# A cross-attention kernel with its instructions in another order: a new table of turns, and a scheduler whose turns need not follow its clock

## The chip, the core and the metric

The kernel runs on one core of one Trainium2 chip. A core has five engines that each work through their own list of instructions in order: TensorE (PE, with its weight loads shown apart as PEld), VectorE (DVE), ScalarE (ACT), GpSimd (POOL) and SyncE (SP, here the main issuer of transfers). They wait for each other through semaphores. The metric is the device time of one execution in microseconds (us). The kernel before has 572.43 us as the median of three runs (572.14 to 574.06).

## The reference

Two attention branches over the same rows are summed, projected and added to the input. `x` is (2, 2048, 640), `enc` (2, 128, 384), with 8 heads of 80 columns; all of it is fp32.

```python
residual = hidden_states                                  # x
enc, ca = encoder_hidden_states[:, :124], encoder_hidden_states[:, 124:]
hs = _mha(hidden_states @ Wq, enc @ Wk, enc @ Wv)         # text branch
ca_q1 = einsum('btc,th->bch', ca, Wq_ca)                  # (2, 384, 640)
ca_q1 = ca_q1[:, indices, :]                              # 2048 rows, 384 different ones
ca_hs1 = _mha(ca_q1, residual, residual)
ca_hs2 = _mha(ca_hs1 @ Wq, ca @ Wk_ca, ca @ Wv_ca)        # adapter branch, 4 tokens
out = (hs + ca_hs2) @ Wout + b_out + residual
```

## The kernel before

The rows are worked in 8 **blocks** of 512 rows (four for each of the two inputs) and 16 **units** of 256 rows. The stages overlap in time:

- **Queries** (`queries_fast`, PE tiles `pq`). The product x·Wq of a block is taken with fewer, larger products in the manner of Strassen: a chain of products accumulates in one PSUM bank, and after each product the running sum is read out and added to a quarter of `q`. Since the next product of a chain goes on in the same bank, it waits until the read of the step before has been done (`ready + at`). The reads are copies on ACT or DVE, or adds on DVE. A fifth column group (`pq_n_4`) is taken plainly; it is split into a rounded half and a rest (ACT cast to `x_sums`, DVE difference, ACT cast to `wq_sums`, DVE difference) and goes to DRAM and back (`away`, `landing`, `rests`).
- **Text scores** (PE tiles `sc`, DVE row maxima `m`, ACT exponentials `p`, transposes `eb`, then through DRAM as `kept` and back as `pT`).
- **The adapter branch**. Scores `s1` come as quads of matmuls into one buffer of four banks. DVE reduces it to maxima (`mx<-s`) and only then may the next quad write; later the scores are taken again (`s<-cop,zop`), ACT makes exponentials `ea`, and PE sums them (`acc<-ea,y_sb`). `y_sb` is x transposed by halves, written to DRAM (`y`) and read back in quarters on the SP queue. The branch ends in 384 rows `o2` for each input (`po2`), kept in DRAM.
- **Text out** (`text_out_fast`, PE tiles `ph` and `po`). For unit m, `ph_m_0`, `ph_m_2` and `ph_m_4` are copied out into `hs` (ACT or DVE), four sums s1 to s4 of parts of `hs` are made on DVE or POOL (s3 from the first copy, s1 from the first two, s2 from s1, s4 from s2), and four chains of products with Wout run in the banks `po_m_0` to `po_m_3`. Chain 0 has four steps. Each step is followed by a DVE add of the bank into the output rows (`x_more` or `last_rows`), and, as with the queries, the next step of a chain waits for that add.
- **Store**. POOL adds the rows of `o2` by an indirect transfer (line 2351), and the output rows are stored by SP or ACT.

An fp32 matmul appears in the trace as two records, so eight matmuls of a chain (two products of `by_columns`, line 405, over four groups of 32 columns) are 16 records.

**What sets the order.** The whole program is written out by a list scheduler, the class `Desk`. Tasks are generators that yield operations (`Do`): the engines that may do it, a function that emits instructions, the events to wait for, and the buffers it takes (`needs`) and gives back (`frees`). The table `TURNS` holds for every operation of every task a number; `run` always issues the operation with the least number, and the number modulo 6 names its engine in `ENGINES` (PE, ACT, DVE, POOL, SP, NONE). Instructions are pinned in this order. So the table alone sets the order on each engine, and where an operation may go to two engines, which one does it. The scheduler keeps a clock of its own with modelled durations (`ready`, `issue`, `streamed`); of that clock one thing reaches the program: which buffer of a set is taken, since the buffer that became free earliest is. What an engine waits for on the chip follows from the data and the buffers.

Of the kernel before, what the change touches and what calls it, by code (L numbers as in the profile page):

```python
# [14 lines left out]
P = 128  # L15
# [44 lines left out]
class Task:  # L60
    def __init__(self, gen, rank, key, more):
        self.gen, self.rank, self.key, self.more, self.last = gen, rank, key, more, Event()
        self.forks, self.ops, self.path = 0, 0, ""


class Desk:
# [242 lines left out]
    def begin(self, gen, rank):  # L309
        name = gen.__name__  # L310
        n = self.begun[name] = self.begun.get(name, -1) + 1
        task = Task(gen, rank, (name, n), 0.0)
        task.last.t = self.now
        self.parent.forks += 1
        task.path = f"{self.parent.path}.{self.parent.forks}"
# [2276 lines left out]
```

## Time and profile before

| | before |
|---|---|
| median of three runs | 572.43 us (572.14 to 574.06) |
| span of the profiled execution | 571.3 us |
| PE busy | 563.6 us, 99% |
| DVE busy | 394.4 us, 69% |
| ACT busy | 286.7 us, 50% |
| POOL busy | 159.8 us, 28% |
| PE clock granted | 9 of 10 or more in every slice |
| bytes moved | 113.21 MB, mean 198 GB/s |

The profiled execution spans 571.3 us, 1.1 us under the median of the runs. Times in the trace count from the start of that span. A row of a timeline gives the start, the length, the engine, the line, the tiles written and read, the shape and how many instructions of that kind came in a row; a bracket at its end gives the idle time ahead of it and what ended it. Matmuls are pipelined, so the length of a row of PE reaches past the start of the next, and the pitch from start to start is the better price. A short wait of PE can be hidden under the modelled ends.

### The profile page before, as it was taken

The page shows a single profiled execution, that of the slowest core. Times are in us where ns is not written, and L with a number is a line of the kernel's source. Part 1 is how long each engine was busy: PE and PEld are TensorE (multiplying, and loading weights), DVE is VectorE, ACT ScalarE, POOL GpSimd, SP SyncE. Part 2 cuts the span into 40 slices and gives each one's busy share as a digit, 9 for nine tenths or more (in the row PEclk, how much of TensorE's full clock was granted, in tenths as well). Part 3 has the DMA queues.
Part 4 walks back from the last instruction along what each step waited for, and adds up shares of the span by engine and source line. Part 5 has one row for each costly group of instructions (what it writes and reads, how often), then busy time and mean ns, then how long its engine had stood idle before and what let it go on. Part 6 is the DMA issues. An engine that isn't in the chain of part 4 may idle for free.

```text
span 571.3 us, 18875 instructions
## 1 busy us (share of the span) xinstructions
PE 563.6 (99%) x8069; PEld 310.0 (54%) x8069; DVE 394.4 (69%) x659; ACT 286.7 (50%) x806; POOL 159.8 (28%) x213
## 2 busy tenths in 40 slices
PE   9999999999999999999999999999999999999997
PEld 8885335455555455466554554554555554445553
DVE  4366999999998577458999999998332213544443
ACT  2021355645566899899876654524554664100000
POOL 9102041114440731100004350531203053045152
PEclk9999999999999999999999999999999999999999
DMA  8998576965968977446746969977476587799888
GB/s 246 211 248 126 139 161 157 172 179 139 211 212 153 215 182 211 146 126 198 233 158 203 316 180 319 245 217 230 96 263 120 164 206 223 248 211 213 258 156 237
DMA packets 145691, 113.21 MB, mean 198 GB/s; under 512 B 82548, under 2 KB 116980, under 8 KB 145608
## 3 DMA queue, kind: packets, MB, share of 16 engines
q1 hardware_dynamic: 137000, 95.10, 60.0%
q0 software_dynamic: 5632, 10.69, 11.7%
q10 hardware_dynamic: 2976, 6.23, 3.2%
q8 instruction: 63, 1.03, 0.8%
q14 instruction: 20, 0.16, 0.1%
HBM read 71.60 MB, written 40.39 MB: 196 GB/s over the span
## 4 chain that ended last, share of the span: by engine, by line
PE 92%; DVE 3%; ACT 3%; DMA 1%; issue 1%; SPq 0%; ACTq 0%; DVEq 0%
PE po L405 27%; PE pq L405 24%; PE sc L396 7%; PE acc L396 7%; PE s L396 7%; PE ph L396 6%; PE pq L396 4%; PE pyz L396 2%; ACT ea L427 2%; DVE mx L427 2%; PE pv L396 1%; PE pk L396 1%; DMA xz<-in_x_dram 1%; ACT p L427 1%; PE pt_wq L410 1%
## 5 line engine op out<-in xcount | busy, mean ns | idle before, releaser
L427 ACT ACTIVATE p<-sc,m 128x124 f32<-128x124 f32 x256 | 90.1, 381 | 43.4 <-DVE m L427 38.4
L427 DVE TENSOR_REDUCE mx<-s 128x4 f32<-128x2048 f32 x48 | 109.0, 2271 | 1.9 <-PE s L396 1.9
L427 ACT ACTIVATE ea<-s 128x2048 f32<-128x2048 f32 x48 | 90.5, 1884 | 31.4 <-PE s L396 30.9
L405 PE MATMUL po<-wout_sums,hs 128*32 128x320 f32 x1024 | 78.5, 434 | 0.1
L405 PE MATMUL po<-wout_sb,hs 128*32 128x320 f32 x928 | 72.4, 433 | 0.0
L427 POOL TENSOR_TENSOR p<-p,r 128x992 f32<-128x992 f32 x17 | 31.4, 1847 | 130.9 <-DVE r L427 130.9
L405 PE MATMUL pq<-xt,wq_sb 128*32 128x256 f32 (+1 forms) x928 | 66.4, 418 | 0.0
L427 DVE TENSOR_TENSOR last_rows<-last_rows,po 128x320 f32<-128x320 f32 x60 | 28.1, 480 | 44.0 <-PE po L405 43.9
L427 ACT ACTIVATION_READ_ACCUMULATOR p<-sc,m 128x1 f32 x256 | 57.0, 223 | 0.0
L427 DVE TENSOR_TENSOR x_more<-x_more,po 128x320 f32<-128x320 f32 x68 | 32.4, 481 | 34.5 <-PE po L405 32.5
L405 PEld LDWEIGHTS po<-wout_sums,hs 128*32 128x32 f32 x1024 | 33.4, 110 | 32.7 <-issue 2.8
L427 DVE TENSOR_REDUCE m<-sc 128x4 f32<-128x496 f32 x64 | 40.8, 663 | 14.1 <-PE sc L396 14.0
L396 PE MATMUL acc<-ea,y_sb 128*32 128x384 f32 (+2 forms) x768 | 50.2, 382 | 0.2 <-ACT ea L427 0.2
L396 PE MATMUL ph<-pT,vpad 128*32 128x256 f32 x768 | 47.9, 381 | 0.0
L405 PEld LDWEIGHTS po<-wout_sb,hs 128*32 128x32 f32 x928 | 30.1, 110 | 28.2 <-issue 1.6
L2351 POOL DMA_INDIRECT x_more<-o,query x17 | 26.6, 1563 | 67.0 <-DVE x_more L427 31.1
L405 PEld LDWEIGHTS pq<-xt,wq_sb 128*32 128x32 f32 x928 | 27.7, 110 | 28.0 <-issue 13.4
L427 ACT COPY hs<-ph 128x512 f32<-128x512 f32 (+1 forms) x25 | 13.4, 551 | 57.7 <-PE ph L396 57.7
L427 DVE STREAM_TRANSPOSE eb<-p 128x1024 f32<-128x1024 f32 x32 | 39.4, 1233 | 1.2 <-POOL p L427 1.1
L396 PEld LDWEIGHTS sc<-kmain,q 64*128 64x128 f32 x512 | 31.8, 187 | 12.6 <-issue 5.8
L427 POOL TENSOR_TENSOR hs<-hs 128x256 f32<-128x256 f32 x31 | 28.9, 1019 | 33.9 <-ACT hs L427 25.6
L396 PE MATMUL sc<-kmain,q 64*128 64x124 f32 x512 | 38.0, 285 | 0.0
(219 smaller groups left out, 835.0 us busy)
## 6 DMA issues: line engine op xcount, KB each, us to landing
kept<-eb SPq DMA_DIRECT2D x32, 512.0 KB
pT<-kept SPq DMA_DIRECT2D x16, 1024.0 KB
landing<-away SPq DMA_DIRECT2D x15, 512.0 KB
xi<-in_x_dram SPq DMA_DIRECT2D x56, 128.0 KB
x_more<-in_x_dram SPq DMA_DIRECT2D x17, 320.0 KB
last_rows<-in_x_dram SPq DMA_DIRECT2D x15, 320.0 KB
y<-yt SPq DMA_DIRECT2D x16, 256.0 KB
y_sb<-y SPq DMA_DIRECT2D x32, 128.0 KB
```

The source lines that it names most:

```text
L396: self.pin(self.nc.tensor.matmul(out, lhsT, rhs, **kw))
L405: self.pin(self.nc.tensor.matmul(out[j : j + 32], lhsT[:, j : j + 32], rhs, **kw))
L410: self.pin(self.nc.tensor.transpose(out, in_, ident))
L427: self.pin(getattr(engine, what)(*args, **kw))
L2351: desk.pin(nc.gpsimd.indirect_dma_start(out=t, out_offset=None, in_=o2_of[b], in_offset=bass.IndirectOffsetOnAxis(ap=query[:, st : st + 1] ...
```

## The change

The operations stay the same: PE has the same 4494 matmuls and transposes before and now, and no wait, copy or transfer is added in the code of any stage. Four things differ.

1. The table `TURNS` has other numbers for nearly every operation. The order of instructions changes on every engine, though the first 95 rows of PE (about the first 65 us) are the same. Some operations change engine: the sums of `hs` go from 31 on POOL and 33 on DVE to 37 and 27; the sums of `x_sums` from 17 on POOL and 7 on DVE to 22 and 2; two copies of `hs` go from ACT to DVE; six stores of output rows go from ACT's queue to SP's.
2. `Task.placed`: in the scheduler, each operation also waits for the last buffer-taking operation (engine NONE) of its task.
3. `run` no longer holds the clock at the time of the operation before, so that turns need not come in the order of time.
4. The modelled streaming rate in `streamed` goes from 1.2 to 1.193.

Points 2 to 4 act on the scheduler's clock alone. They add no wait on the chip; through the clock they can only change which buffer of a set is taken.

```diff
-        self.forks, self.ops, self.path = 0, 0, ""
+        self.forks, self.ops, self.path, self.placed = 0, 0, "", None
...
-        ".8.4": [703], ".8.5": [935, 1003, 1064, 1069, 1334], ".8.5.1": [1174], ".8.5.2": [1258], ".8.5.3": [1301],
+        ".8.4": [703], ".8.5": [935, 1003, 1064, 1069, 1142], ".8.5.1": [1306], ".8.5.2": [1414], ".8.5.3": [1433],
...
@@ begin
+        task.placed = self.parent.placed
@@ go_on
         op.wait = [task.last] if op.after is None else [self.event(k) for k in op.after]
+        if task.placed is not None:
+            op.wait.append(task.placed)
+        if op.engines == ("NONE",):
+            task.placed = op.at
@@ run
-            self.issue(max(self.ready(op), self.free[engine], self.now), engine, op)
+            self.issue(max(self.ready(op), self.free[engine]), engine, op)
@@ streamed
-        return (max(n / 1.2, 106 if self.mode[1] > 32 else 27) + (9 if self.mode == (64, P) else 2.5)) / 1e3
+        return (max(n / 1.193, 106 if self.mode[1] > 32 else 27) + (9 if self.mode == (64, P) else 2.5)) / 1e3
```

Line numbers of the changed kernel are those of before plus 5 (405 becomes 410). Three places show what the new table moves. In the rows below a name is the tile written, then those read; `po_15_0` is the bank of chain 0 of unit 15, and `x8` stands for eight matmuls.

**The end of the program.** PE before, its last rows:

```order
L405 MATMUL po_15_0_7039<-wout_sb_100,hs_0_4130 32x320 x8
L405 MATMUL po_8_0_6951<-wout_sb_100,wout_sums_4129 32x320 x4
L405 MATMUL po_8_3_7054<-wout_sb_100,hs_2_5064 32x320 x8
L405 MATMUL po_8_3_7054<-wout_sb_100,wout_sums_4129 32x320 x4
L405 MATMUL po_15_2_7069<-wout_sb_100,hs_0_4130 32x320 x12
L405 MATMUL po_15_0_7039<-wout_sums_4129,hs_0_4130 32x320 x8
L405 MATMUL po_15_3_7094<-wout_sb_100,hs_0_4130 32x320 x12
L405 MATMUL po_15_1_7110<-wout_sums_4129,hs_0_4130 32x320 x8
L405 MATMUL po_15_0_7039<-wout_sums_4129,hs_0_4130 32x320 x8
L405 MATMUL po_15_1_7110<-wout_sums_4129,hs_0_4130 32x320 x8
L405 MATMUL po_15_1_7110<-wout_sb_100,hs_0_4130 32x320 x4
L405 MATMUL po_15_0_7039<-wout_sb_100,hs_0_4130 32x320 x4
```

PE now, its last rows:

```order
L410 MATMUL po_15_1_7055<-wout_sums_4114,hs_2_5028 32x320 x8
L410 MATMUL po_15_0_7067<-wout_sb_100,hs_2_5028 32x320 x8
L410 MATMUL po_15_0_7067<-wout_sums_4114,hs_2_5028 32x320 x8
L410 MATMUL po_15_1_7055<-wout_sums_4114,hs_2_5028 32x320 x8
L410 MATMUL po_15_1_7055<-wout_sb_100,wout_sums_4114 32x320 x4
L410 MATMUL po_15_0_7067<-wout_sums_4114,hs_2_5028 32x320 x8
L410 MATMUL po_15_3_7113<-wout_sb_100,hs_2_5028 32x320 x8
L410 MATMUL po_15_3_7113<-wout_sb_100,wout_sums_4114 32x320 x4
L410 MATMUL po_15_0_7067<-wout_sb_100,wout_sums_4114 32x320 x4
L410 MATMUL po_15_2_7138<-wout_sb_100,hs_2_5028 32x320 x8
L410 MATMUL po_15_2_7138<-wout_sb_100,wout_sums_4114 32x320 x4
```

and DVE now, near its end, the adds of the same chains:

```order
L432 TENSOR_TENSOR last_rows_4223<-last_rows_4223,po_8_1_6967 128x320
L432 TENSOR_TENSOR last_rows_4223<-last_rows_4223,po_8_0_6956 128x320
L432 TENSOR_TENSOR x_more_3020<-x_more_3020,po_15_1_7055 128x320
L432 TENSOR_TENSOR x_more_3020<-x_more_3020,po_8_2_7042 128x320
L432 TENSOR_TENSOR x_more_3020<-x_more_3020,po_8_3_6987 128x320
L432 TENSOR_TENSOR last_rows_4223<-last_rows_4223,po_15_0_7067 128x320
L432 TENSOR_TENSOR x_more_3020<-x_more_3020,po_15_0_7067 128x320
L432 TENSOR_TENSOR x_more_3020<-x_more_3020,po_15_1_7055 128x320
```

Before, 28 matmuls of other chains stood between the first product of `po_15_0` and its second. Now its second product follows the first at once, and the add that lies between them stands on DVE behind the adds of `po_15_1`, `po_8_2` and `po_8_3`.

**Unit 14, chain 0.** PE before:

```order
L405 MATMUL po_12_0_6335<-wout_sums_4129,hs_2_5064 32x320 x8
L405 MATMUL po_12_2_6537<-wout_sb_100,hs_2_5064 32x320 x8
L405 MATMUL po_12_2_6537<-wout_sb_100,wout_sums_4129 32x320 x4
L405 MATMUL po_14_2_6554<-wout_sb_100,hs_1_4229 32x320 x8
L405 MATMUL po_14_2_6554<-wout_sb_100,wout_sums_4129 32x320 x4
L405 MATMUL po_14_0_6568<-wout_sb_100,hs_1_4229 32x320 x8
L405 MATMUL po_12_1_6398<-wout_sums_4129,hs_2_5064 32x320 x8
L405 MATMUL po_12_1_6398<-wout_sb_100,wout_sums_4129 32x320 x4
L405 MATMUL po_12_0_6335<-wout_sb_100,wout_sums_4129 32x320 x4
L405 MATMUL po_14_0_6568<-wout_sums_4129,hs_1_4229 32x320 x8
```

PE now:

```order
L401 MATMUL pt_p2_1_6439<-ident_69,p2_1_6361 32x128 x8
L401 MATMUL ph_14_0_6453<-pT_14_6408,vpad_1_108 32x256 x8
L401 MATMUL po2_1_0_6464<-w2_sb_110,p2T_1_6448 128x320 x4
L401 MATMUL ph_14_2_6471<-pT_14_6408,vpad_1_108 32x256 x8
L401 MATMUL ph_14_4_6480<-pT_14_6408,vpad_1_108 32x256 x8
L401 MATMUL po2_1_1_6493<-w2_sb_110,p2T_1_6448 128x320 x2
L410 MATMUL po_12_0_6399<-wout_sums_4114,hs_1_4141 32x320 x8
L410 MATMUL po_14_0_6511<-wout_sb_100,hs_0_4129 32x320 x8
L410 MATMUL po_14_1_6524<-wout_sums_4114,hs_0_4129 32x320 x8
L410 MATMUL po_14_0_6511<-wout_sums_4114,hs_0_4129 32x320 x8
```

and DVE now, from the first copy of the unit on:

```order
L432 COPY hs_0_4129<-ph_14_0_6453 128x512
L432 COPY o2_1_6463<-po2_1_0_6464 128x640
L432 COPY hs_0_4129<-ph_14_2_6471 128x512
L432 TENSOR_TENSOR hs_0_4129<-hs_0_4129 128x256
L432 TENSOR_TENSOR last_rows_4223<-last_rows_4223,po_12_0_6399 128x320
L432 TENSOR_TENSOR hs_1_4141<-hs_1_4141 128x256
L432 TENSOR_TENSOR x_more_3020<-x_more_3020,po_14_0_6511 128x320
L432 TENSOR_TENSOR hs_1_4141<-hs_1_4141 128x256
```

Before, 32 matmuls of units 12 and 14 stood between the last `ph` of the unit and the first product of `po_14_0`, and 16 between its first and its second. Now the `ph` of the unit are interleaved with `po2_1`, 10 matmuls stand ahead of the first product and 8 between the two, and the copies into `hs_0` share DVE with a copy of `o2_1`. The sums s3, s1 and s2 of the unit are made on POOL; DVE's sum of `hs_0` in the fourth row is s4, and the add of `po_14_0` comes behind it.

**Block 3, chain 0 of the queries.** PE now, up to the start of the score group `sc_0_5` (16 matmuls in 16 rows):

```order
L410 MATMUL pq_3_4_1518<-xt_0_3_1114,wq4_99 32x512 x8
L410 MATMUL pq_3_0_1501<-x_sums_891,wq_sums_850 32x256 x16
L410 MATMUL pq_3_4_1518<-xt_0_3_1114,wq4_99 32x512 x4
L401 MATMUL sc_0_5_0_1599<-kmain_105,q_1_653 128x124
L401 MATMUL sc_0_5_1_1600<-kmain_105,q_1_653 128x124
```

PE now, from the last row of that group on:

```order
L401 MATMUL sc_0_5_1_1600<-krest_106,rests_841 128x124
L401 MATMUL s1_0_2_0_1_1628<-zop_0_2_1193,cop_153 128x512 x4
L410 MATMUL pq_3_0_1501<-x_sums_891,wq_sums_850 32x256 x16
L410 MATMUL pq_3_1_1659<-xt_0_3_1114,wq_sb_98 32x256 x16
L401 MATMUL s1_0_2_1_0_1677<-zop_0_2_1193,cop_153 128x512 x4
```

and ACT now, at the same place:

```order
L432 ACTIVATE p_0_837,r_0_4_1547<-sc_0_4_0_1527,m_0_4_0_1545 128x4x31 x4
L432 ACTIVATE p_0_837,r_0_4_1547<-sc_0_4_1_1528,m_0_4_1_1546 128x4x31 x4
L432 CAST x_sums_891<-pq_3_4_1518 128x256
L432 CAST wq_sums_850<-pq_3_4_1518 128x256
L432 COPY q_3_1500<-pq_3_0_1501 128x2x256
L432 ACTIVATE p_1_838,r_0_5_1619<-sc_0_5_0_1599,m_0_5_0_1617 128x4x31 x2
L432 CAST zop_0_3_1484<-zs_0_3_1_1589 128x512
```

Before, a quad and the same score group stood between these two products of `pq_3_0` too, but ACT's copies of `pq_3_0` stood between exponentials, and the casts of `pq_3_4` came later, behind them. Now the copy that the second product of `pq_3_0` waits for stands behind the two casts of `pq_3_4`, the second of which waits for DVE's difference.

392 rows, old and new, of the table TURNS are left out of this document.

## Prediction

> **What bounds the kernel now.** I read the page's head and its chain of waits first, then PE's waits, then the span by stretches.
>
> ```profile
> span 571.3 us, 18875 instructions
> PE 563.6 (99%) x8069; PEld 310.0 (54%) x8069; DVE 394.4 (69%) x659; ACT 286.7 (50%) x806; POOL 159.8 (28%) x213
> PE 92%; DVE 3%; ACT 3%; DMA 1%; issue 1%; SPq 0%; ACTq 0%; DVEq 0%
> ```
>
> PE is busy for 563.6 of 571.3 us and makes 92% of the chain. The change gives PE the same matmuls, so the time can move only by PE's waits. PE's own waits are few:
>
> ```profile
> PE unread L396 <- DVE zeros L427: 1.1, 1, 1.1
> PE s L396 <- DVE mx L427: 1.1, 2, 0.7
> PE s L396 <- ACT ea L427: 0.6, 3, 0.2
> ...
> PE acc L396 <- ACT ea L427: 0.2, 1, 0.2
> ```
>
> The columns are us in total, times, and the longest. The first row belongs to the start of the program, which keeps its order. So what can be seen to be won is 1.1 + 0.6 + 0.2 = 1.9 us, and everything else that the new order does can only add waits or uncover hidden ones. The stretches (start:end, length, then PE, PEld, DVE, ACT and POOL busy, the granted clock, the transfers' share and GB/s) say where:
>
> ```profile
> 200.00:240.00 40.00, 40.00 (x647) 21.28 (x645) 26.37 (x46) 36.81 (x88) 8.06 (x5) 1.00 0.69 185
> 240.00:280.00 40.00, 39.43 (x662) 24.63 (x659) 29.83 (x44) 39.34 (x113) 1.28 (x1) 1.00 0.59 190
> 300.00:340.00 40.00, 38.75 (x558) 20.31 (x560) 39.25 (x45) 24.33 (x97) 17.30 (x15) 1.00 0.80 240
> 500.00:540.00 40.00, 40.00 (x631) 20.61 (x627) 17.82 (x42) 2.34 (x4) 14.54 (x13) 1.00 0.89 221
> ```
>
> ACT is full (39.34 of 40) in the stretch in which `ea` is late, DVE is full (39.25 of 40) where `mx` is late; after 500 us both have time to spare, and PE does not wait at all. The granted clock is 1.00 in each, so it gives nothing to win.
>
> The profiled execution stands 572.43 - 571.3 = 1.1 us under the median of the runs. I make the sum against the span and add 1.1.
>
> **The change part by part.** *The quads that wait for `mx`.*
>
> ```profile
> 305.82 0.50 PE L396 MATMUL s<-zop,cop 32*128 32x512 f32 x4
> 307.13 1.91 PE L396 MATMUL ph<-pT,vpad 128*32 128x256 f32 x32
> 309.49 0.51 PE L396 MATMUL s<-zop,cop 32*128 32x512 f32 x4 [0.45 <-DVE mx L427]
> 313.15 0.50 PE L396 MATMUL s<-zop,cop 32*128 32x512 f32 x4 [0.66 <-DVE mx L427]
> 307.16 2.27 DVE L427 TENSOR_REDUCE mx<-s 128x4 f32<-128x2048 f32 x1
> 310.86 2.23 DVE L427 TENSOR_REDUCE mx<-s 128x4 f32<-128x2048 f32 x1
> ```
>
> A quad may write only when the reduction (2.27 us) of the quad before has been read. The quads stood 3.67 and 3.66 us apart with too little PE work between them: 0.45 and 0.66 us of waiting. In the new order the quad `s1_1_1_0_0` follows 24 matmuls of `ph` and a score group, and the next one follows 40 matmuls of `po`; by the pitch of the `ph` row (1.91 us for 16 matmuls, so 2.9 for 24) both have over 4 us of cover, and this pair of waits goes. But the table has close quads elsewhere (`s1_0_2_1_1` and `s1_1_2_1_0`, one score group or little more between), where DVE must be quick. I book one wait of 0.4, the nearest being the 0.45 above: -1.1 + 0.4 = -0.7. Bounds: -1.1 (no new wait) and +0.2 (two of 0.66 instead).
>
> *The waits for `ea`.* These 0.8 us come where ACT is full. The new order has the same exponentials there and fewer copies in between on ACT. I book half, -0.4; bounds -0.8 and 0.
>
> *The end.* Chain 0 of unit 15: between two products of `po_15_0` lies a DVE add.
>
> ```profile
> 562.62 3.44 PE L405 MATMUL po<-wout_sums,hs 128*32 128x320 f32 x48
> 565.85 1.29 PE L405 MATMUL po<-wout_sb,hs 128*32 128x320 f32 x16
> 553.74 1.28 DVE L427 TENSOR_TENSOR last_rows<-last_rows,po 128x320 f32<-128x320 f32 x3 [2.35 <-PE po L405]
> L427 DVE TENSOR_TENSOR x_more<-x_more,po x68: 433/486/490, 317.5 to 567.2; 128x320 f32<-128x320 f32 x68
> ```
>
> 48 records of PE start 3.23 us ahead of the next row, so eight matmuls (16 records) take 1.08 us. One add takes 0.49 us, and three in a row 1.28, so 0.40 for each that follows another. Before, 28 matmuls stood between the two products (3.8 us). Now none: PE does the first product of `po_15_0` (1.08 us) while DVE does the adds of `po_15_1`, `po_8_2` and `po_8_3`; the add that PE wants is the fourth. From the end of `po_15_1`'s product: 0.1 to start, 3 x 0.40, 0.49, and 0.1 to 0.2 back to PE: 1.9 to 2.0. Less the cover of 1.08 that is +0.9. Bounds: +0.3 if `po_8_2`, `po_8_3` were not ahead, +1.2 with slower hand-over. Behind the waiting product stand all the other products of the program, so nothing hides it. The stores behind the last add cost as before (two short issues and a landing), booked at 0.
>
> *Unit 14, chain 0.* What PE waits for now is a line of seven operations on DVE and POOL.
>
> ```profile
> L427 DVE COPY hs<-ph x12: 417/688/692, 326.2 to 538.6; 128x512 f32<-128x512 f32 x11, 128x256 f32<-128x256 f32 x1
> L427 DVE TENSOR_TENSOR hs<-hs x33: 381/419/1661, 333.2 to 548.1; 128x256 f32<-128x256 f32 x33
> 506.31 2.00 POOL L427 TENSOR_TENSOR hs<-hs 128x256 f32<-128x256 f32 x2
> 492.26 0.82 DVE L427 COPY o<-po 128x640 f32<-128x640 f32 x1 [0.38 <-ACT o L427]
> ```
>
> From the end of `ph_14_2`: its copy on DVE 0.69 (the copy of `o2_1`, 0.82, is ahead of it but runs during `ph_14_2`), s1 and s2 on POOL 2.00, s4 on DVE 0.42, the add of `po_12_0` 0.40, a sum of `hs_1` 0.42, the add of `po_14_0` 0.49: 4.4, and some six hand-overs of 0.1 to 0.2 give 5.0 to 5.6. PE meanwhile has `ph_14_4` (1.0), a pair of `po2_1_1` (an estimate of 0.3), and three times eight matmuls at 1.08: 4.5. I book +0.9. Bounds: 0 if POOL's sums run at the 0.7 that its quickest take, +2 if one sum is held as long as the 1661 ns that DVE's longest took.
>
> *Block 3, chain 0 of the queries.*
>
> ```profile
> 143.73 0.37 ACT L427 CAST x_sums<-pq 128x256 fp32r<-128x256 f32 x1 [1.77 <-PE pq L405]
> 145.83 0.37 ACT L427 CAST wq_sums<-pq 128x256 fp32r<-128x256 f32 x1 [1.21 <-DVE x_sums L427]
> L427 ACT COPY q<-pq x24: 570/586/623, 32.1 to 295.9; 128x512 f32<-128x512 f32 x24
> 310.93 1.16 PE L396 MATMUL sc<-kmain,q 64*128 64x124 f32 x16
> 311.84 0.65 PE L396 MATMUL sc<-krest,rests 64*128 64x124 f32 x8
> ```
>
> ACT's copy of `pq_3_0` stands behind two casts, and the second cast waits for DVE. The casts came 2.10 us apart here; with DVE at once it is 0.37 + 0.40 + hand-over, 0.9. To the next cast's end and the copy: 0.9 to 2.1, + 0.37 + 0.59 + 0.3 = 2.2 to 3.4 us. PE has the score group (0.91 + 0.6) and a quad (0.44): 1.95. So 0.2 to 1.4; I take +0.6, nearer the low end, since in the new order no `mx` stands between the two differences on DVE.
>
> *`y_sb` on SP's queue.* The fourth quarter of `y_sb` moves from ahead of the first `kept_7` to behind it.
>
> ```profile
> 216.16 0.58 SPq L447 DMA_DIRECT2D y_sb<-y  x1
> 220.09 0.67 SPq L447 DMA_DIRECT2D kept<-eb  x1
> 226.04 1.07 PE L396 MATMUL acc<-ea,y_sb 128*32 128x384 f32 x16
> DMA to landing us min/median/max: 4.9/5.3/9.6
> ```
>
> `kept` waits for DVE's transpose and was issued at 220.09; with it and the load of `w2_sb` ahead, `y_sb` goes out near 221.7 instead of 216.16. The shortest landing in the last row (that of the `o` transfers, the nearest that I have) makes 226.6, and the first product that reads this quarter ran at 226.04. Booked +0.5; bounds 0 and, with the longest landing, +5.
>
> *The rest.* PE's changes of tile shape go from 262 to 263, +0.1. The twelve more sums on POOL, the six stores that go from ACT's queue to SP's and the two copies that go from ACT to DVE are booked at nothing: they lie beside PE in stretches where DVE and POOL have time left (17.82 and 14.54 of 40 us). If that cover were gone, each would cost its own length, 0.5 to 1.3. The clock edits in the scheduler add no instruction: nothing.
>
> Sum: -0.7 - 0.4 + 0.9 + 0.9 + 0.6 + 0.5 + 0.1 = +1.9, so a span of 573.2 and, with 1.1 and rounding, a time of **574.4**.
>
> **The rivals.** *(a) Faster.* PE's waits of 1.9 go and the chains cost nothing, because PE comes to them later than I reckon (DVE and POOL then lead by more). For it: DVE is busy for 17.82 of 40 us late in the program, so a lead is cheap there. Against: the end has no cover in the order itself. 572.4 - 1.9 = 570.5, and a little less if waits hidden under modelled ends go too.
>
> *(b) No change.* Removed waits are 1.9 instead of 1.1, and of the four new ones only the end and one half of the others bite: -1.9 + 0.9 + 1.0 = 0.0, so 572.4. It would also be so if the change did not do what it says, only renaming buffers; but the rows of the order differ on every engine.
>
> *(c) Much slower: a transfer decides.* If `y_sb` takes the long landing of 9.6 us, PE waits at its `acc` for 221.7 + 9.6 - 226.04 = 5.3 us: 572.4 + 5.3 + 1.4 (the other terms) = 579. It decides from a landing of 4.3 us on. Against: between 200 and 240 us the transfers are at 0.69 of their time, not full.
>
> *(d) POOL holds DVE.*
>
> ```profile
> 395.50 1.84 POOL L427 TENSOR_TENSOR p<-p,r 128x992 f32<-128x992 f32 x1 [10.30 <-DVE r L427]
> 395.96 1.66 DVE L427 TENSOR_TENSOR hs<-hs 128x256 f32<-128x256 f32 x1
> ```
>
> A DVE sum of 0.42 us that started inside a sum of POOL took 1.66 and ended 0.28 after POOL's. Twelve more two-input operations go to POOL. If two of those hold an operation on which a chain waits, 2 x 1.24 more: 574.4 + 2.5 = 576.9. The Trainium skill's "SBUF — State Buffer" (the rule on the shared port pair) says that a DVE operation with two SBUF inputs and a GpSimd operation that reads SBUF exclude each other for a whole instruction; by that rule, with which these two rows agree, moving sums to POOL frees less of DVE than their length. The adds of `po` read PSUM and would not be held.
>
> **How the numbers follow.** The forecast's own range is 573.3 to 576.0 with a chance of 0.40. (a) has 0.20, (b) 0.27, (c) 0.07, (d) 0.06. What a measurement of this kernel can tell from no change is 0.3%, 1.7 us: 570.7 to 574.1. Of the forecast's 0.40, 0.08 lies under 574.1. Faster: 0.20. Same: 0.27 + 0.08 = 0.35. Slower: 0.32 + 0.07 + 0.06 = 0.45. The range for 8 in 10 goes from 570.0 (half of what (a) can give beyond its waits) to 577.4 (past (d), short of (c)).
>
> **What would show it.** Right: in PE's waits the row `s <- DVE mx` at 0.4 or less; a new row of `po` waiting for `last_rows` near the last 6 us (0.9), one for `hs` or `x_more` some 60 us before the end (0.9), one of `pq <- ACT q` near 137 us (0.2 to 1.4), one of `acc` behind a transfer of `y_sb` near 226 us. Wrong: PE busy all through the last 40 us; or a wait of PE over 2 us on a transfer; or a busy sum of PE that differs by more than 1 us, which would mean that shapes or the clock, not waits, made the difference.

## The result

The changed kernel takes **576.75 us**, median of four runs (575.31 to 578.07); the kernel before takes 573.09 (four runs, 572.14 to 574.06: the three from above and one more). The ratio is **1.0065**, with an interval of 1.0047 to 1.0082: slower, by about 3.7 us. The forecast was 574.4 with a range of 570.0 to 577.4, and slower as the likeliest side.

The profiled execution is the quickest of the four: span 573.3 us, time 575.31. The spans of the others are 575.3, 574.4 and 576.0. So two things must be read apart: what stands in this one profile, and what differs from run to run. A second profile of the same kernel (span 575.5, time 577.36; called *the second profile* below) shows the other end.

The page's row of busy times and the chain of waits, after:

```profile
PE 563.7 (98%) x8069; PEld 307.3 (54%) x8069; DVE 394.2 (69%) x650; ACT 285.2 (50%) x805; POOL 171.3 (30%) x223
PE 69%; DVE 15%; ACT 6%; DMA 5%; issue 4%; SPq 2%; DVEq 0%; ACTq 0%
```

PE is as busy as before (563.7 against 563.6 us), so the work did not change in length. But PE makes 69% of the chain instead of 92%: DVE, ACT and transfers now often set what comes next. PE's waits after (total, times, longest):

```profile
PE pq L410 <- ACT p L432: 1.3, 1, 1.3
PE unread L401 <- DVE zeros L432: 1.1, 1, 1.1
PE s L401 <- DVE mx L432: 0.9, 4, 0.3
PE pq L410 <- DVE wq_sums L432: 0.8, 1, 0.8
PE po L410 <- DVE last_rows L432: 0.7, 1, 0.7
PE s L401 <- ACT ea L432: 0.5, 2, 0.4
PE pq L410 <- ACT q L432: 0.3, 1, 0.3
```

The second row is that of the start and stands in both kernels. New are the waits of `pq` (1.3, 0.8, 0.3) and of `po` (0.7). The stretches tell where the time went; the columns are those of the prediction's table of stretches. Before:

```profile
130.00:185.00 55.00, 55.00 (x832) 29.98 (x834) 52.61 (x70) 31.73 (x139) 18.38 (x14) 1.00 0.76 180
300.00:500.00 200.00, 198.60 (x3006) 101.00 (x3008) 128.38 (x193) 102.34 (x245) 59.84 (x51) 1.00 0.76 216
```

After:

```profile
130.00:185.00 55.00, 53.62 (x840) 31.00 (x841) 54.04 (x63) 32.95 (x141) 20.34 (x15) 1.00 0.74 169
300.00:500.00 200.00, 199.59 (x3068) 102.78 (x3064) 131.01 (x197) 104.76 (x261) 62.73 (x55) 1.00 0.74 217
```

Length less PE's busy time is PE's idle time. From 130 to 185 us DVE went from 52.61 to 54.04 of 55 us, and PE, which had been busy all through, now idles for 1.38. DVE as a whole did not get more work: from 50 to 185 us it is busy for 127.5 of 135 us in both profiles, and the new order moves 1.4 us of that behind 130 us. From 300 to 500 us PE's idle time fell from 1.40 to 0.41. The same subtraction, in us, for the kernels that matter below (those that are not named yet are the experiments):

| PE idle in | before | after | second profile | y_sb first | kept first | kept and y_sb first | SP order | old to 185 us | old first half |
|---|---|---|---|---|---|---|---|---|---|
| 50 to 185 | 0.00 | 1.93 | 1.91 | 1.92 | 1.94 | 2.29 | 1.90 | 0.00 | 0.19 (50 to 200) |
| 185 to 200 | 0.18 | 0.19 | 1.01 | 1.12 | 0.00 | 0.00 | 0.00 | 0.18 | in the row above |
| 200 to 300 | 0.57 | 1.88 | 2.22 | 2.78 | 1.06 | 0.78 | 1.76 | 1.11 | 0.70 |
| 300 to 500 | 1.40 | 0.41 | 0.43 | 0.43 | 0.44 | 0.43 | 0.45 | 0.43 | 0.43 |
| 500 to 565 | 0.00 | 0.73 | 0.73 | 0.64 | 0.88 | 1.02 | 0.73 | 0.73 | 0.74 |

Against before, the first row and the last two are nearly the same in every run of the whole new order: some +1.9 (2.3 once), -1.0 and +0.7 (0.6 to 1.0). The second and third rows differ from run to run and make 1.2 of the 2.2 us between the two profiles of the change. Not all of the spread is in this table: up to 180 us every engine has the same list in the changed kernel and in the kernels of "y_sb first" to "SP order", and yet the same product of block 3 (the row at 131.86 below) starts at 131.86 us after, 132.48 in the second profile, and at 132.40, 133.51 and 132.90 with kept first, with kept and y_sb first and in the SP order. So a difference of 1 us between two single profiles can be the run and not the order; the times of many runs decide. Together with the tail of stores behind PE's last product (below, -0.9) the column "after" gives +1.93 + 0.01 + 1.31 - 0.99 + 0.73 - 0.9 - 0.2 (the first 50 us) = +1.9, and the two profiled spans differ by 2.0.

### The profile page after: what moved, and what is told of

Same layout as the page of the kernel before. It is cut to its first block, busy times and chain, and to the rows that moved or that the text cites. A ratio compares the mean times of both kernels' runs of the same rounds, so it can differ in the third digit from the quotient of the medians.

```text
span 573.3 us, 18888 instructions
## 1 busy us (share of the span) xinstructions
PE 563.7 (98%) x8069; PEld 307.3 (54%) x8069; DVE 394.2 (69%) x650; ACT 285.2 (50%) x805; POOL 171.3 (30%) x223
## 4 chain that ended last, share of the span: by engine, by line
PE 69%; DVE 15%; ACT 6%; DMA 5%; issue 4%; SPq 2%; DVEq 0%; ACTq 0%
PE po L410 25%; PE pq L410 11%; PE ph L401 6%; PE acc L401 6%; DVE mx L432 6%; PE s L401 5%; PE pq L401 4%; PE sc L401 3%; ACT ea L432 3%; DMA kept<-eb 2%; ACT p L432 2%; SPq L452 2%; DVE eb L432 2%; DVE m L432 1%; DVE xt L432 1%
## 5 line engine op out<-in xcount | busy, mean ns | idle before, releaser
L432 POOL TENSOR_TENSOR p<-p,r 128x992 f32<-128x992 f32 x18 | 33.2, 1843 | 173.7 <-DVE r L432 167.3
L410 PE MATMUL po<-wout_sb,hs 128*32 128x320 f32 x992 | 76.5, 433 | 0.0
L432 DVE TENSOR_TENSOR last_rows<-last_rows,po 128x320 f32<-128x320 f32 x64 | 30.3, 484 | 51.9 <-PE po L410 51.8
L432 DVE TENSOR_TENSOR x_more<-x_more,po 128x320 f32<-128x320 f32 x64 | 29.9, 480 | 33.2 <-PE po L410 32.9
L432 POOL TENSOR_TENSOR hs<-hs 128x256 f32<-128x256 f32 x37 | 32.1, 874 | 64.3 <-DVE hs L432 37.0
L410 PEld LDWEIGHTS po<-wout_sums,hs 128*32 128x32 f32 x1024 | 31.3, 110 | 34.3 <-issue 3.5
L410 PEld LDWEIGHTS po<-wout_sb,hs 128*32 128x32 f32 x992 | 31.4, 110 | 32.4 <-issue 1.5
L401 PE MATMUL ph<-pT,vpad 128*32 128x256 f32 x768 | 46.5, 380 | 0.0
L2356 POOL DMA_INDIRECT last_rows<-o,query x16 | 25.1, 1568 | 53.7 <-DVE last_rows L432 44.5
L410 PE MATMUL pq<-xt,wq 128*32 128x512 f32 x280 | 34.1, 595 | 0.1
```

Source lines behind the costliest of these rows:

```text
L401: self.pin(self.nc.tensor.matmul(out, lhsT, rhs, **kw))
L410: self.pin(self.nc.tensor.matmul(out[j : j + 32], lhsT[:, j : j + 32], rhs, **kw))
L432: self.pin(getattr(engine, what)(*args, **kw))
L2356: desk.pin(nc.gpsimd.indirect_dma_start(out=t, out_offset=None, in_=o2_of[b], in_offset=bass.IndirectOffsetOnAxis(ap=query[:, st : st + 1] ...
```

## The experiments

All ratios are against runs of the kernel before on the same chip. "Old" is the table of before, "new" that of the change; line numbers are those of the changed kernel. The table can be cut: the first part of its 2281 operations in one order and all others in the other's order is again a valid program, though at the cut each engine meets a joint that neither kernel has.

**The scheduler's edits alone, and the order by halves**

```diff
 clock_only: TURNS = old; task.placed, run and streamed as in the change
 new_first:  TURNS = new for the first 1200 operations (to about 286 us), then the rest in old order
 new_last:   TURNS = old for the first 1200 operations (to about 277 us), then the rest in new order
```

> The old table of turns under the new scheduler: the order of every engine is that of before, only the choice of buffers can differ. My theory (the order makes the loss): within 0.3% of before, 572 to 574 us. Rival (the edits of the scheduler's clock choose worse buffers, and that makes part of the loss): 1 us or more slower than before.

> The new order for the first half of the operations (about the first 286 us of PE's work), the old order for the rest. My theory (PE waits of 0.3 and 0.8 us at the queries of blocks 3 and 4, and of 1.3 us near 227 us behind a late transfer on SP's queue, all in the first half): 2 to 3 us slower than before. Rival (the loss lies in the chains of text out and the stores, in the second half): within 1 us of before.

> The old order for the first half of the operations (about 277 us), the new order for the rest. My theory: the wait of 0.7 us at the end less the waits for the maxima that go: within 1 us of before. Rival (the loss lies in the second half): 2 to 3 us slower than before.

Measured: clock_only 573.3 us, ratio 0.9997 (0.9988 to 1.0007): points 2 to 4 of the change cost and bring nothing. new_first 581.36 us, 1.014 (1.011 to 1.0171). new_last **572.27 us, 0.9978 (0.997 to 0.9987)**: the second half of the new order is a gain of about 1.2 us, and this splice beats both kernels. In new_last's waits of PE stand:

```profile
PE po L410 <- DVE last_rows L432: 0.7, 1, 0.7
PE s L401 <- DVE mx L432: 0.4, 2, 0.2
```

The wait at the end is there with its 0.7 and the quads are at 0.4, both as I had booked them; there is no `pq` row. new_first is no clean measure of the first half: all its runs are 5 us and more above before, in two groups (578.8 to 579.5 and 583.3 to 583.8), and its joint brought waits of its own:

```profile
PE s L401 <- DVE mx L432: 3.1, 5, 1.5
```

The quads' 3.1 us in total are more than in any other of these kernels, and the longest of them, 1.52 us, stands at 286.52, where the two orders meet. So the two halves must not be added; that the loss lies in the first half follows from new_last alone.

**Where in the first half**

```diff
 new_from_185: TURNS = old for the first 800 operations (to about 185 us), then new
 new_from_150: TURNS = old for the first 600 operations (to about 150 us), then new
```

> The old order for the first third of the operations (to about 185 us of PE's work), the new order for the rest; SP's queue between 205 and 230 us is that of the changed kernel. Theory (the steady part of the loss is a row of short waits of PE between 60 and 185 us, 2.6 us in sum by the two traces; the spread between runs comes from SP's queue after 200 us): about 2.5 us faster than the changed kernel, near before, but with the changed kernel's spread of 2 us and more. Rival (the loss is the late transfers after 200 us alone): as slow as the changed kernel.

> The old order to about 150 us, the new order for the rest. Theory (by the traces 1.3 us of short waits lie between 90 and 150 us and 1.3 us between 150 and 185 us): half way between the changed kernel and the kernel with the old order to 185 us, 1.002 to 1.004 of before. Rival (all of it lies at the queries of block 4 near 160 us): as slow as the changed kernel.

Measured: new_from_185 573.13 us, 1.0004 (0.9994 to 1.0014). Against the second measurement of the change (after_again, 1.0058, below) some 0.54%, 3.1 us, come back when the order up to 185 us is the old one. Its runs spread over 2.9 us (572.25 to 575.10), those of new_last, which keeps the old order to 277 us, over 1.0. And its ratio lies above that of new_last (0.9978) by 0.26%, with intervals that do not meet: the new order from 185 to 277 us costs some 1.5 us as well, even behind an old beginning. In thirds the change is thus about +3.1, +1.5 and -1.2 us, with the reserve that each splice has a joint. new_from_150 took 581.33 us, 1.0157 (1.0137 to 1.0178), and says nothing on the place: the joint itself stalls. DVE's row and PE's at the joint:

```profile
154.38 1.25 DVE L432 STREAM_TRANSPOSE eb<-p 128x1024 f32<-128x1024 f32 x1 [5.63 <-DMA kept<-eb]
152.36 3.36 PE L410 MATMUL pq<-xt,wq 128*32 128x512 f32 x16 [2.17 <-ACT p L432]
```

A transpose waits 5.63 us for a transfer to have read its buffer, and all of DVE's list stands behind it. That is the same kind of wait as the next experiments are about, only larger.

**Transfers on SP's queue, 185 to 300 us.** In the profile of after the longest wait of PE, 1.29 us at 228.01, goes back to this on SP and DVE (SP's issues, then DVE's two transposes into `eb`):

```profile
215.11 2.61 SPq L452 DMA_DIRECT2D xi<-in_x_dram  x2
...
219.49 0.56 SPq L452 DMA_DIRECT2D kept<-eb  x1
```

```profile
212.93 1.24 DVE L432 STREAM_TRANSPOSE eb<-p 128x1024 f32<-128x1024 f32 x1
224.63 1.25 DVE L432 STREAM_TRANSPOSE eb<-p 128x1024 f32<-128x1024 f32 x1 [2.83 <-DMA kept<-eb]
```

The `kept` transfer, whose data were ready at 214.2, was issued only at 219.49, behind loads of `xi`. DVE's next transpose into that buffer waited 2.83 us for it; behind the transpose stood the row maximum `m`, behind that ACT's `p`, and behind that the bank that the next `pq` takes. In the trace of before DVE waits for no `kept` and no `z`. In new_from_185 `kept` stands behind the same loads (issued at 216.71, 5.2 us after its data), but DVE waits only 1.10 us for it and the wait of `pq` is not there: the late issue alone does not stop PE. Three kernels tell `kept` from `y_sb`, which my prediction had named:

```diff
 kept_first, SP:   DMA kept_6<-eb_6_0   moved ahead of the six loads xi_1_3<-in_x_dram before it
 ysb_first, SP:    DMA y_sb<-y_0_3      moved from behind kept_7 and w2_sb to ahead of kept_7
 kept_ysb, SP:     both
```

> The changed kernel with one move on SP's queue: the transfer of the sixth unit's transposed probabilities (kept_6 from eb_6_0) is issued ahead of the last six loads of x of its block instead of behind them. My theory: the transfer leaves 4 to 5 us earlier, DVE's next transpose no longer waits 2.8 us for its buffer, and PE's wait of 1.3 us near 227 us goes: 1 to 2 us faster than the changed kernel, with less spread between runs. Rival (that wait is hidden or replaced by a wait for the loads of x, which now come later): the time of the changed kernel within 0.5 us.

> The changed kernel with one move on SP's queue: the fourth quarter of y_sb is issued ahead of the first kept_7 and the load of w2_sb instead of behind them. Theory (in some runs this quarter lands after PE wants it, which makes the spread of 2.7 us between runs): the lowest runs stay, the highest come down, a median 1 us under the changed kernel's. Rival (kept_6 behind the loads of x makes the spread): no difference to the changed kernel.

> The changed kernel with both moves on SP's queue, kept_6 ahead of the last six loads of x and y_sb ahead of kept_7. Theory: both late transfers go, 1.5 to 2.5 us faster than the changed kernel with a spread under 1.5 us; what stays are the short waits before 185 us, so still 1 to 2 us slower than before. Rival (the transfers only move the wait elsewhere): the time of kept_6 alone, within 0.5 us.

Measured: kept_first 576.03 us, 1.0043 (1.0028 to 1.0057); ysb_first 576.87, 1.0064 (1.0049 to 1.0079); kept_ysb 575.77, 1.0039 (1.0026 to 1.0053). Moving `y_sb` brings nothing in the times, although PE's wait for it (0.29 in kept_first) is gone in kept_ysb. Moving `kept` took the wait away: `kept` goes out ahead of the loads, at 214.75 instead of 219.49, and the row of DVE's next transpose into `eb` (222.29, 1.24 us) has no bracket.

```profile
214.75 0.56 SPq L452 DMA_DIRECT2D kept<-eb  x1
```

PE's row `pq <- ACT p` is gone too, and PE idles 1.06 and 0.78 us from 200 to 300 us instead of 1.88 to 2.78. By the times that is worth some 0.2% (1.0043 and 1.0039 against 1.0058 to 1.0065), with intervals that overlap: a part of the loss at best, not its whole.

**The same kernel again, and SP's order mended in three places**

```diff
 after_again: no edit
 sp_order, SP: as kept_ysb, and z_1_0<-zs_1_0_0 moved ahead of the last three loads xi_1_2<-in_x_dram
```

> The changed kernel itself, once more, beside the three others and more runs of before. If the loss is steady: a ratio of 1.005 to 1.008 to before, with runs spread over 2 to 3 us.

> The changed kernel with three moves on SP's queue: the last three loads of x of one block go behind the transfer z from zs (they stood ahead of it near 182 us), kept_6 ahead of the last loads of x of the next block, y_sb ahead of kept_7. Theory (transfers queued behind bunched loads of x make both the wait near 227 us and the one near 198 us that only some runs have): 1.5 to 2.5 us faster than the changed kernel beside it, and no wait of DVE for z or kept. Rival (the spread has another cause): 0.5 us faster or less, and the spread stays.

Measured: after_again 576.27 us, 1.0058 (1.0045 to 1.0071); sp_order 576.23, 1.0051 (1.0038 to 1.0064). The second profile shows other waits of PE than the first:

```profile
199.47 1.95 PE L401 MATMUL pyz<-xt,wyz 64*32 64x512 f32 x32 [1.01 <-DVE wq_sums L432]
208.63 1.07 PE L401 MATMUL acc<-ea,y_sb 128*32 128x384 f32 x16 [0.82 <-ACT ea L432]
232.45 1.07 PE L401 MATMUL acc<-ea,y_sb 128*32 128x384 f32 x16 [0.46 <-DMA y_sb<-y]
```

The wait at 229.6 is 0.17 here instead of 1.29, but 1.01 and 0.82 have come up 30 and 20 us earlier, and `y_sb` costs the 0.46 that it did not cost in the first profile. The 1.01 goes back to `z`. DVE shuffles into the buffer `zs`, the transfer `z` empties it, and the next shuffle waits until that has been done:

```profile
188.55 0.57 SPq L452 DMA_DIRECT2D z<-zs  x1
193.82 0.01 DVE L432 LOAD_MASK_SELECT zs<-yz  x1 [4.51 <-DMA z<-zs]
194.62 0.34 SPq L452 DMA_DIRECT2D z<-zs  x1
```

The first shuffle ended at 186.39. Its `z` was issued at 188.55, behind `xi` loads, `y`, `y_sb` and `kept`, and DVE went on at 193.82, 5.3 us after the issue; the second `z` could only follow the second shuffle. In the first profile the same `z` was issued at 186.27, and DVE went on at 190.06, after 3.8 us, with a wait of 1.39. One `xi` load, issued in 2.34 us at 182.41 instead of 0.67 at 181.14, makes most of the later issue. Before, the two shuffles stood 16 us apart; `z` was issued still later, 11 us after the first, and DVE did not wait for it:

```profile
170.24 0.74 DVE L427 STREAM_SHUFFLE zs<-yz 128x512 f32<-128x512 f32 x1
181.79 0.49 SPq L447 DMA_DIRECT2D z<-zs  x1
186.67 0.01 DVE L427 LOAD_MASK_SELECT zs<-yz  x1
```

So it is DVE's new order, with shuffles at 185.01 and 190.08 after, that lets `z` be waited for. The 0.82 goes back to another transfer: ACT's cast of `landing` stands ahead of the `ea` that PE wants, and waits for it (0.49 us in the first profile):

```profile
206.18 0.62 ACT L432 CAST rests<-landing 128x512 fp32r<-128x512 f32 x1 [1.66 <-DMA landing<-away]
```

sp_order did shorten DVE's waits for `z` and `kept` (4.5 and 2.2 us in the second profile), and DVE waited for the loads in their place:

```profile
DVE xt L432 <- DMA xi<-in_x_dram: 2.9, 2, 1.8
DVE zs L432 <- DMA z<-zs: 0.8, 2, 0.6
DVE eb L432 <- DMA kept<-eb: 0.6, 1, 0.6
```

ACT's cast still waits 1.70 us for `landing`, and PE 0.86 for `ea`. The time is that of the change. Whatever goes first on SP in this stretch, something behind it is late; this repair moves the wait, it does not remove it.

**The casts, 130 to 165 us**

```diff
 casts_late, ACT: COPY q_3<-pq_3_0 moved ahead of both casts of pq_3_4;
                  COPY q_4<-pq_4_0 moved ahead of the second cast of pq_4_4
 casts_late, DVE: both differences of pq_4_4 moved ahead of the transposes eb_3_1 and xt_1_1
 casts_late, SP:  the transfer of kept that waits for that eb moved behind two loads of y_sb
```

> The changed kernel with two moves near 131 and 160 us: ACT's copies of pq_3_0 and pq_4_0 go ahead of the casts of pq_3_4 and of the second cast of pq_4_4, and DVE takes both differences of pq_4_4 ahead of a transpose of eb and one of xt. Theory (PE's waits of 0.3 and 0.8 us come from the order of these reads): both waits go, 0.7 to 1.1 us faster than the changed kernel beside it. Rival (DVE is full there, so the delayed transposes and maxima give the time back): within 0.4 us.

Measured: 578.11 us, 1.0094 (1.0071 to 1.0118), slower still. The waits of `pq` for `q` and for `wq_sums` are gone from PE, and the quads pay:

```profile
PE s L401 <- DVE mx L432: 2.6, 4, 1.9
```

PE idles 2.04 us from 130 to 185 us instead of 1.38 (its busy time there is 52.96). So these waits are not two copies in a bad place: DVE has no time left there, and what is put first makes the next one late. The time is not made by waits alone: four of the six runs have a mean granted clock of 0.997, and they are the slowest (578.00 to 580.44); the two at 1.000 took 575.78 and 577.43, like the changed kernel. What the clock did is in the last section.

**The end**

```diff
 last_end = new_last, and on PE: po_15_3 x12 moved between the first and the second product of po_15_0;
            po_15_2 x12 (with its DVE add) moved ahead of the last x4 of po_15_0
```

> The old order for the first half and the new order for the second, with one more move: 12 matmuls of po_15_3 stand between the first and the second product of po_15_0, and those of po_15_2 ahead of its last. Theory (PE's last wait is the add between two products that follow each other): PE's wait for last_rows of 0.7 us goes, 0.4 to 0.8 us faster than the same splice without the move (0.9978 of before), so 0.996 to 0.997 of before. Rival (the end waits for the stores): no difference.

Measured: 572.69 us, 0.999 (0.9979 to 1.0), against 0.9978 for new_last without this move: no gain. PE's wait for `last_rows` is gone (PE is busy for all of the 65 us from 500 to 565), but the span is 570.8 instead of 570.5. The very last store, in last_end:

```profile
567.18 0.46 ACTq L452 DMA_DIRECT2D out_dram<-last_rows  x1
```

and in new_last:

```profile
567.69 0.34 ACTq L452 DMA_DIRECT2D out_dram<-last_rows  x1
```

In last_end it was the third store within 0.9 us (the others were issued at 566.71 and 566.75), and 3.1 us followed to the end of the span (570.78 - 567.64); in new_last it came alone, 0.4 us later, and 2.5 followed (570.49 - 568.03). Of the 0.7 won on PE, 0.4 reached the last store, and in these two profiles the end gave it back. How firm that is stands in the last section.

## Why the prediction came out as it did

The sign was right, and the predicted span (573.2) is within 0.1 of the profiled one. That closeness is luck: several terms were off and cancelled. Of the waits booked for unit 14 (0.9) and for `y_sb` (0.5) none came in this profile; 0.77 in block 4 and 1.29 behind `kept`, which stood in no term, took their place.

**From the span to the time: mis-sized.** I added 1.1 us around the span (573.2 + 1.1 is 574.3, not 574.4), from a profiled span and a median of other runs. Each of the four runs has its own span and time, and they differ by 1.8 to 2.1. That is 0.9 of the 2.35 us that the forecast was short. The rest is that the sum agrees with the quickest run, while the typical one has a span of 574.4 or 575.3. Where those runs lose more is not recorded; in the second profile, of span 575.5, 0.6 of the 2.2 us more had come by the product at 131.86, and 2.1 by the quad that starts at 241.17 (there at 243.29).

**The quads (`mx`, booked -0.7): right after 300 us, mis-sized as a whole (-0.2: 1.1 became 0.9).** After 300 us the waits of 0.45 and 0.66 are gone and these two have come, 0.4 together as booked:

```profile
354.79 0.51 PE L401 MATMUL s<-zop,cop 32*128 32x512 f32 x4 [0.18 <-DVE mx L432]
384.88 0.50 PE L401 MATMUL s<-zop,cop 32*128 32x512 f32 x4 [0.23 <-DVE mx L432]
```

By the stretches that part gained 1.0. The other half of the row of 0.9, 0.28 at 117.55 and 0.17 at 164.17, comes from the full DVE early on, for which I had no term.

**`ea` (booked -0.4): about right.** 0.8 became 0.5.

**The end (booked +0.9): right on PE, wrong in what followed it.** The line I named is in the trace:

```profile
560.55 1.28 DVE L432 TENSOR_TENSOR x_more<-x_more,po 128x320 f32<-128x320 f32 x3 [2.21 <-PE po L410]
561.75 0.48 DVE L432 TENSOR_TENSOR last_rows<-last_rows,po 128x320 f32<-128x320 f32 x1
570.10 0.49 DVE L432 TENSOR_TENSOR last_rows<-last_rows,po 128x320 f32<-128x320 f32 x1 [1.13 <-PE po L410]
```

```profile
562.29 2.36 PE L410 MATMUL po<-wout_sums,hs 128*32 128x320 f32 x32 [0.73 <-DVE last_rows L432]
```

Three adds, then the one that PE wants: 0.73. The hand-overs of 0.1 to 0.2 in my sum stand in no row: this add ended at 562.23 and PE started at 562.29, 0.06 later. But the failed step is the sentence that the stores behind the last add cost as before. Before:

```profile
566.66 1.03 DVE L427 TENSOR_TENSOR x_more<-x_more,po 128x320 f32<-128x320 f32 x2 [0.61 <-PE po L405]
```

From the end of this pair, 567.69, to the end of the span were 3.6 us; after, from 570.59 (the last add, the row at 570.10), 2.7. The new order ends on a single add and store, and between these two profiles the end became 0.9 shorter. The size is not firm: clock_only ends in the order of before, and from its last add, at 568.38, to the end were 2.9. So the 0.73 on PE was paid back by 0.2 to 0.9; last_end shows from the other side that removing it brings no gain.

**Unit 14 (booked +0.9): wrong, 0.** The chain is there, and PE does not wait:

```profile
503.80 1.54 POOL L432 TENSOR_TENSOR hs<-hs 128x256 f32<-128x256 f32 x2 [1.46 <-DVE hs L432]
505.37 0.42 DVE L432 TENSOR_TENSOR hs<-hs 128x256 f32<-128x256 f32 x1 [1.65 <-POOL hs L432]
506.44 0.48 DVE L432 TENSOR_TENSOR x_more<-x_more,po 128x320 f32<-128x320 f32 x1
```

The two sums on POOL took 1.54, and DVE went on 0.03 us after them; I had booked 2.00 and hand-overs of 0.1 to 0.2 (the sums are 0.77 each, near the bound of 0.7 at which I had said that nothing is left). The add ended at 506.92, and the product that wants it comes after the first half of the 32 records that start at 506.16, near 507.2.

**Block 3's queries (booked +0.6): mis-sized, 0.28.** But the pattern comes again in block 4, which I had not priced, and there costs 0.77:

```profile
131.86 1.93 PE L410 MATMUL pq<-x_sums,wq_sums 128*32 128x256 f32 x32 [0.28 <-ACT q L432]
162.06 1.93 PE L410 MATMUL pq<-xt,wq_sums 128*32 128x256 f32 x32 [0.77 <-DVE wq_sums L432]
```

```profile
158.93 1.22 DVE L432 STREAM_TRANSPOSE eb<-p 128x1024 f32<-128x1024 f32 x1
160.07 0.67 DVE L432 STREAM_TRANSPOSE xt<-xi 128x512 f32<-128x512 f32 x1
160.67 0.39 DVE L432 TENSOR_TENSOR x_sums<-pq,x_sums 128x256 fp32r<-128x256 f32 x1
161.49 0.42 DVE L432 TENSOR_TENSOR wq_sums<-pq,wq_sums 128x256 fp32r<-128x256 f32 x1 [0.44 <-ACT wq_sums L432]
```

Two transposes stand ahead of the first difference. These two, the quads' waits there (0.62 in all) and two of 0.13 make the 1.9 us from 50 to 185 us, against the 0.6 booked. This is the largest steady error: I followed the diff at three places, and the loss lay in many small ones in a stretch where DVE is full.

**`y_sb` on SP's queue (booked +0.5): the right queue, the wrong transfer.** In the profile of after it cost 0, in the second one 0.46, and ysb_first brought nothing. What was late were `kept`, `z` and `landing`, which I had not followed: 1.29 us for `kept` in the first profile; 1.01 for `z`, 0.82 for `landing` and 0.17 for `kept` in the second.

**The rivals.** (a), faster: wrong for the whole; new_last shows the sign for the second half, though there too the end cost its 0.7. (b), no change: wrong, though of the scheduler's edits alone it is true (clock_only). (c): PE never waited 5 us on `y_sb`; that PE would wait behind transfers was right, by another path (DVE's buffers) and at a smaller price. (d): in unit 14 POOL's sums ran at 0.77 and DVE's sum behind them at 0.42; the longest sum of `hs` on DVE took 1.42, at 377.08, and PE waited for nothing near it.

**What is not settled.** That most of the loss comes from the order before 185 us is shown by new_from_185 (3.1 us come back). How these 3.1 split is not: 1.9 are PE's idle time up to 185 us, steady in every run, and the rest fits the waits behind late transfers from 185 to 300 us, which are smaller behind the old beginning (DVE waits 1.1 and 0.5 us for `kept` and `z`). That DVE's late list is what makes those transfers bite is argued from these waits, not tested by itself. Why one `xi` load took 2.34 us to issue in one run and 0.67 in another, and why DVE had to wait 5.3 us from the issue of `z` instead of 3.8, I cannot say.

## What to carry to other kernels

When an order is changed everywhere, do not price only the places where the diff looks close: look first for the stretches in which a helper engine is nearly full (here DVE at 54 of 55 us) and follow every operation there, with the transfers that free its buffers. The fullness by itself is no loss: the old order had DVE at 52.6 of the same 55 us and no wait of PE. A store that frees a buffer can stand behind loads on the same queue, and one issued 5.3 us after its data were ready (`kept`) reached the main engine through two others. New orders can be spliced: half of this one is better than either whole.

## What the hardware showed that I had not expected

**Behind some short waits of PE the clock fell.** In casts_late PE waited 1.90 us for the quad at 165.15, and the products behind it ran at 2.93 us instead of 1.93; the granted clock from 165 to 170 us is 0.66, and 0.50 from 167 to 169.

```profile
165.15 0.51 PE L401 MATMUL s<-zop,cop 32*128 32x512 f32 x4 [1.90 <-DVE mx L432]
165.59 2.93 PE L410 MATMUL pq<-x_sums,wq_sums 128*32 128x256 f32 x32
```

```profile
165.00:170.00 5.00, 4.85 (x52) 2.26 (x53) 4.13 (x6) 3.47 (x17) 1.30 (x1) 0.66 0.35 113
```

The next quad started 4.85 us later, at 170.00; in the changed kernel the same stretch, from 164.17 to 167.53, took 3.36. So the fall cost 1.5 us beyond the wait. In new_from_150 it came twice. The row behind the wait of 2.17 took 3.36 (shown above), where the same form took 1.92 some 5 us later, with a clock of 0.50 from 153 to 156 us; and a second time near 166.5, where waits of 1.47 and 1.01 us stood 3 us apart and the clock from 167 to 169 is 0.50:

```profile
166.71 3.42 PE L410 MATMUL pq<-xt,wq_sums 128*32 128x256 f32 x32 [1.01 <-DVE wq_sums L432]
```

But behind waits of 1.55 and 1.52 us in new_first, of 1.29 after and of 1.01 in the second profile the clock stayed at 1.00. So the length of one wait does not decide; what does, these runs do not show. The Trainium skill's "TensorE: Matmul & The Clock Gate" (What's actually happening) puts the fall of the clock after at least one idle window of about 3.4 us; these two runs show a fall behind shorter waits.

**The end of the span is not a fixed price.** Behind the issue of the last store 2.35 to 2.47 us followed in the ten profiles that end on one store alone (after and new_last among them). Where two or three were issued within a microsecond it was more, but not by a steady amount: 3.25 (before), 3.1 (last_end), 2.9 (new_first) and 2.55 (clock_only, which ends in the order of before).
